# Thirty of 2,346 gathered tiles fetched row by row on SP's queue

## The chip, the core and the metric

The kernel runs on one core of one Trainium2 chip. The metric is the device time of one execution in microseconds (us). The kernel before was run three times: 2960.32, 2960.99 and 2961.77 us, median 2960.99.

## What is computed

The reference is a three-layer graph network over 6,250 nodes of 256 features and 100,000 edges in three relations, and the edges are sorted by their destination. Cut to what matters:

```
ew = edge_attr @ edge_w + edge_b                        # 100000 x 256, the same in all layers
for l in range(3):
    msg = relu(x[src] * ew)                             # one gathered row of x for each edge
    out = x @ roots[l] + biases[l]
    for i in range(3):
        h = segment_sum(msg * (type == i)[:, None], dst, n) * inv_cnt[i][:, None]
        out = out + h @ weights[l, i]
    x = x + relu(out)
result = layernorm(x_in + x)
```

The expression `x[src]` is the point of the change: in each layer 100,000 rows of 1 KB are read from DRAM at addresses that only the data tells. Layer 0 reads them from the input x, layers 1 and 2 from `x_mid`, the layer's input that the layer before wrote to DRAM.

## The kernel before, in words

The edges are cut into tiles of 128, one edge in each partition: 782 tiles a layer. Two tiles are a pair, two pairs a quad; a layer has 391 pairs. The order of the pairs is a list, `order`: pairs 64 to 390 first, then 63 down to 0. The kernel is written as a hand-made software pipeline (`layer`, from L587): a loop over steps `it`, one pair a step, in which each kind of work on a pair is issued at a fixed distance. Every engine keeps the order in which its instructions are written.

- **Gather**, nine steps ahead (AHEAD, called `gather`). `gather_pair` (L1051) issues one indirect DMA for each tile from GpSimd (POOL): 128 rows by 128 indices, L1054. The quad's four tiles go to one of eight rooms of a ring (`rows`, ROWS = 8). The first six pairs of a layer are fetched at the end of the layer before, from a copy of the nodes in which one node tile is still missing, and completed later.
- **Edge weights**, five steps ahead: TensorE (PE) multiplies the edge attributes with `edge_w` (L634). The attributes come by `load_at`, a 256 KB load from SP's queue for every eight pairs (L571), into three rooms.
- **Messages**, three steps ahead: VectorE (DVE) multiplies the gathered quad with the weights (L656), ScalarE (ACT) takes the relu (L657).
- **Sums**, at the step itself: PE multiplies the messages with one-hot matrices (L687, L695), DVE adds the result into an accumulator (`add`, L723) at a place that is loaded into registers, eight at once (L716). After that the quad's room is free.
- **Nodes**: when all edges of a node tile (128 nodes) are in, PE multiplies its sums with the weights (`node_mul`, L754), DVE ends it (`node_end`, L785, L788) and SP stores it to `x_mid` (L791), in the last layer to the output (L808). The first of these node tiles come some 15 steps apart, the last ones four.

So SP's queue holds the attribute loads, the weight loads, in the last layer loads of the input (L815), and the stores. It waits at each store until DVE has made it.

At the start of layer 0 ACT's queue loads the biases and zeroes parts of the accumulator, writes zeros to `x_mid` (L526) and loads the node features six tiles at a time (`load_x`, L557), the first of them ahead of the loop. At step 20 `find_came` and `find_rows` (L574, L580) make the index tables of the later layers.

Of the kernel before, what the change touches and what calls it, by code (L numbers as in the profile page):

```python
# [442 lines left out]
def ordered_path(ctx, tc, x, attr_laid, A, weights, roots, biases, edge_w, edge_b, out, src, src_i, seg, place_i, consts, x_root,  # L443
# [6 lines left out]
    nc = tc.nc  # L450
    P = 128
    N, D = x.shape
    E = src.shape[0]
# [9 lines left out]
    order, _, _, least, most = schedule(N, E, 1)  # L463
# [15 lines left out]
    big = ctx.enter_context(tc.tile_pool(name="big", bufs=1))  # L479
# [47 lines left out]
    src_r = big.tile(list(src_i.shape), I32, name="src_r")  # L527
    src_e = big.tile([P, 2 * FIRST], I32, name="src_e")
    came = big.tile([P, 2 * FIRST, P], F32, name="came")
    came_i = came.bitcast(I32)  # L530

    edge = ctx.enter_context(tc.tile_pool(name="edge", bufs=2))
    rows = ctx.enter_context(tc.tile_pool(name="rows", bufs=ROWS))
    wpool = ctx.enter_context(tc.tile_pool(name="wpool", bufs=1))
    o_pool = ctx.enter_context(tc.tile_pool(name="o_p", bufs=1, space=PSUM))
    r_pool = ctx.enter_context(tc.tile_pool(name="r_p", bufs=1, space=PSUM))
# [3 lines left out]
    def first_of(p, n):  # L540
        return p == 0 or order[p - 1] // n != order[p] // n
# [8 lines left out]
    def closes(u):  # L550
        p = order.index(u)
        return p == U - 1 or span_of[order[p + 1]] != span_of[u]

    def load_x(c0):
        n = min(6, NT - 1 - c0)
        if n > 0:
            nc.scalar.dma_start(x_all[:, c0:c0 + n, :], x[c0 * P:(c0 + n) * P, :].rearrange("(c p) d -> p c d", p=P))  # L557
        if c0 + 6 >= NT - 1:
            last = N - (NT - 1) * P
            nc.scalar.dma_start(x_all[:last, NT - 1, :], x[N - last:, :])  # L560
# [13 lines left out]
    def find_rows():  # L574
        mine = src_i[:, 2 * order[0]:2 * (order[0] + FIRST)]
        for to, of, there in ((src_r, src_i, N + P), (src_e, mine, N)):
            nc.vector.tensor_scalar(to, of, float(P), float(there), op0=ALU.is_lt, op1=ALU.mult)
            nc.vector.scalar_tensor_tensor(to, of, float(-P), to, op0=ALU.add, op1=ALU.add)

    def find_came():  # L580
        e = 2 * P * order[0]
        nc.scalar.dma_start(came_i.rearrange("p t e -> p (t e)"),
                            src[e:e + 2 * FIRST * P][None, :].to_broadcast([P, 2 * FIRST * P]))
        for t in range(2 * FIRST):
            nc.vector.tensor_scalar(came[:, t, :], came_i[:, t, :], node_i[:, 0:1], None, op0=ALU.is_equal)

    def layer(l, r_sb, b_sb, ats, early, pools):  # L587
# [4 lines left out]
        _, starts, moved, _, _ = schedule(N, E, share)  # L592
# [9 lines left out]
        seen, h_bank = [0], {}  # L602

        def gather(u):
            p = order.index(u)
            if p < FIRST:
                xs[u // 2] = early[u // 2]
            else:
                if first_of(p, 2):
                    xs[u // 2] = room(rows, D)  # L610
                gather_pair(nc, xs[u // 2], x_rows, src_i if l == 0 else src_r, u)

        def pairs_of(q):
            return range(min(2, U - 2 * q))
# [207 lines left out]
        for j, c in enumerate(turns_of):  # L822
            step = max(3 + int((U - 110) * (1 - (1 - j / NT) ** 0.5)), max(root_at, default=-1) + 6)
            if j >= ROOTS:
                step = max(step, starts[turns_of[j - ROOTS]] + 5)
            assert step + 8 <= starts[c]
            root_at[step] = c
        for it in range(-11, max(starts) + 8):
            def pair(k):
                return order[it + k] if 0 <= it + k < U else None  # L830
            if pair(AHEAD) is not None:
                gather(pair(AHEAD))
            if l < L - 1 and 0 <= it + AHEAD - U < FIRST:
                gather_early(it + AHEAD - U)
            if l == 0 and it == 20:
                find_came()
                find_rows()
            if pair(AHEAD) is not None and pair(AHEAD) // GROUP not in ats:
                ats[pair(AHEAD) // GROUP] = load_at(pair(AHEAD) // GROUP)
            if l == 0 and it >= -4 and (it + 4) % 20 == 0 and (it + 4) // 20 * 6 < NT - 1:  # L840
                load_x((it + 4) // 20 * 6)
            if it == 10:
                nc.sync.dma_start(w_sb, weights[l].rearrange("r (c p) e -> p (r c) e", p=P))
            if l == L - 1 and it + 2 in root_at:
                load_x0(root_at[it + 2])
            if l < L - 1 and it == U - 10:
                r_next = load_root(l + 1)
            if l < L - 1 and U - 10 <= it < U - 8:
                ats_next[at_groups[it - U + 10]] = load_at(at_groups[it - U + 10])

            if pair(0) is not None:
                reduce(pair(0))
            for span in take_at.get(it, ()):
                take(span)
            if pair(5) is not None and first_of(it + 5, 2):
                make_ew(pair(5) // 2)
            for span in turn_at.get(it, ()):
                turn(span)
            if pair(3) is not None and first_of(it + 3, 2):
                if l > 0 and it + 3 < FIRST:  # L860
                    complete(pair(3) // 2)
                if pair(3) // 2 != order[-1] // 2:
                    weigh(pair(3) // 2)

            if pair(3) is not None and pair(3) // 2 == order[-1] // 2:
                k = pair(3) % 2
                if pair(3) == order[-1]:
                    weigh_last(pair(3) // 2, k)
                else:
                    weigh(pair(3) // 2, range(k, k + 1))  # L870
            if pair(6) is not None and first_of(it + 6, 2):
                seed_ew(pair(6) // 2)
            if it - 6 in root_at:
                root_keep(root_at[it - 6])
            if it in root_at:
                root_turn(root_at[it])
            if it - 2 in root_at:
                root_turned(root_at[it - 2])
            if it - 3 in root_at:
                root_mul(root_at[it - 3])  # L880
            if it == moved:
# [47 lines left out]
OCT = 4  # L929
PARTS = 3  # L930
FIRST = 6

ASTRAY = 1024

# [113 lines left out]
    return rows.tile([128, 2, 2, D], F32, name="xs", bufs=ROWS)  # L1048


def gather_pair(nc, xs, x_rows, src_i, u, u0=0):  # L1051
    for i in range(2):
        t = 2 * (u - u0) + i
        nc.gpsimd.indirect_dma_start(  # L1054
            out=xs[:, u % 2, i, :], out_offset=None, in_=x_rows[:, :],
            in_offset=bass.IndirectOffsetOnAxis(ap=src_i[:, t:t + 1], axis=0))
# [169 lines left out]
```

## Time and profile before

| | |
|---|---|
| Median of three runs | 2960.99 us |
| Profiled execution, its own time | 2962.1 us |
| Span of the profiled execution, first to last instruction | 2959.9 us |
| Mean granted TensorE clock | 0.972 |
| Busy share of PE, DVE, ACT, POOL | 87%, 68%, 51%, 75% |
| Indirect DMAs of L1054 on POOL | 12 + 770 + 24 + 1540 = 2,346 |
| Mean rate of all DMA | 131 GB/s |

How to read it: the profile lists busy time by engine; a share says how much of the span the engine worked and not whether it holds the others up. Instructions that set registers, wait or issue a DMA do not count as busy; they are listed under the names of the sequencers, SPq, ACTq, POOLq and DVEq. An indirect DMA counts on POOL with the time in which POOL makes its descriptors, and not with the time in which the rows travel. In a row of a timeline the last part, in brackets, is how long the engine was idle before the instruction and what ended that.

### The profile page before, as it was taken

The page shows a single profiled execution, that of the slowest core. Times are in us where ns is not written, and L with a number is a line of the kernel's source. Part 1 is how long each engine was busy: PE and PEld are TensorE (multiplying, and loading weights), DVE is VectorE, ACT ScalarE, POOL GpSimd, SP SyncE. Part 2 cuts the span into 40 slices and gives each one's busy share as a digit, 9 for nine tenths or more (in the row PEclk, how much of TensorE's full clock was granted, in tenths as well). Part 3 has the DMA queues.
Part 4 walks back from the last instruction along what each step waited for, and adds up shares of the span by engine and source line. Part 5 has one row for each costly group of instructions (what it writes and reads, how often), then busy time and mean ns, then how long its engine had stood idle before and what let it go on. Part 6 is the DMA issues. An engine that isn't in the chain of part 4 may idle for free. (4 is left out here: it accounts for less than half of the span.)

```text
span 2959.9 us, 43407 instructions
## 1 busy us (share of the span) xinstructions
PE 2585.9 (87%) x13712; PEld 1779.5 (60%) x13712; DVE 1999.4 (68%) x4910; ACT 1503.9 (51%) x1911; POOL 2227.8 (75%) x2355
## 2 busy tenths in 40 slices
PE   5999999999998778888889998778888988999876
PEld 2566677677765545556666666455555666666644
DVE  6666677778775555566767776545566777888864
ACT  4666666566565444454444444434444444444443
POOL 7777777777777777777777777777777777777776
PEclk9999999999999999999999999989999999999998
DMA  5444444444444444444444444444444444444443
GB/s 168 146 146 136 148 124 124 129 131 129 129 133 130 132 116 120 129 122 123 127 125 130 131 131 129 135 132 125 125 133 134 135 132 132 138 136 139 129 127 96
DMA packets 173705, 387.39 MB, mean 131 GB/s; under 512 B 43594, under 2 KB 79068, under 8 KB 173468
## 3 DMA queue, kind: packets, MB, share of 16 engines
q0 software_dynamic: 112608, 307.65, 36.4%
q1 hardware_dynamic: 53280, 68.50, 7.2%
q10 hardware_dynamic: 7580, 8.37, 1.0%
q8 instruction: 113, 1.85, 0.3%
q14 instruction: 124, 1.02, 0.1%
HBM read 364.89 MB, written 19.46 MB: 130 GB/s over the span
## 5 line engine op out<-in xcount | busy, mean ns | idle before, releaser
L1054 POOL DMA_INDIRECT xs<-x_mid,src_r x1540 | 1460.3, 948 | 469.1 <-issue 360.0
L657 ACT ACTIVATE xs<-xs 128x1024 f32<-128x1024 f32 (+1 forms) x585 | 615.7, 1052 | 1290.2 <-DVE xs L656 1269.8
L656 DVE TENSOR_TENSOR xs<-ew_p,xs 128x1024 f32<-128x1024 f32 (+1 forms) x585 | 711.8, 1217 | 662.0 <-DMA xs<-x_mid,src_r 433.4
L1054 POOL DMA_INDIRECT xs<-in_x_dram,src_io x770 | 731.2, 950 | 235.4 <-issue 196.8
L695 PEld LDWEIGHTS h_p<-oh,xs 128*128 128x128 f32 x5160 | 665.1, 195 | 253.7 <-issue 122.5
L695 PE MATMUL h_p<-oh,xs 128*128 128x120 f32 x5160 | 728.9, 286 | 88.7 <-issue 38.2
L634 PE MATMUL ew_p<-ew_sb,at 64*128 64x512 f32 x2346 | 688.5, 663 | 106.0 <-ACT ew_p L621 101.1
L669 DVE TENSOR_SCALAR oh<-iota_w,seg_o 128x120 f32<-128x120 f32 x2346 | 623.5, 328 | 0.0
L687 PE MATMUL h_p<-xs,oh 128*120 128x256 f32 x2088 | 571.7, 408 | 21.4 <-issue 7.4
L621 ACT ACTIVATE ew_p<-seed 128x1024 f32<-128x1024 f32 x582 | 588.8, 1012 | 0.0
L754 PE MATMUL o_p<-w_sb,acc 128*128 128x256 f32 (+1 forms) x1728 | 440.1, 391 | 30.5 <-DVE x_root L785 27.4
L687 PEld LDWEIGHTS h_p<-xs,oh 128*120 128x120 f32 x2088 | 363.7, 192 | 163.1 <-issue 50.0
L723 DVE TENSOR_TENSOR acc<-h_p,acc 128x240 f32 (+1 forms) x732 | 324.6, 443 | 184.8 <-PE o_p L754 67.9
L754 PEld LDWEIGHTS o_p<-w_sb,acc 128*128 128x128 f32 (+1 forms) x1728 | 309.4, 191 | 152.2 <-DVE x_root L785 67.3
L634 PEld LDWEIGHTS ew_p<-ew_sb,at 64*128 64x128 f32 x2346 | 182.0, 189 | 234.7 <-ACT ew_p L621 131.0
L785 DVE SCALAR_TENSOR_TENSOR x_root<-o_p,inv,x_root 128x256 f32<-128x256 f32 (+1 forms) x432 | 207.3, 480 | 27.6 <-PE o_p L754 20.9
L736 PE MATMUL r_p<-r_sb,t_s 128*128 128x256 f32 x588 | 160.8, 397 | 25.3 <-ACT t_s L732 25.0
L771 ACT ACTIVATE acc<-zero_o 128x768 f32<-128x768 f32 (+1 forms) x150 | 140.2, 935 | 15.2 <-PE o_p L754 14.6
L673 ACT ACTIVATE oh_b<-oh 128x480 bf16<-128x480 f32 x196 | 116.4, 594 | 59.0 <-DVE oh L669 58.1
L736 PEld LDWEIGHTS r_p<-r_sb,t_s 128*128 128x128 f32 x588 | 104.6, 195 | 46.2 <-ACT t_s L732 34.5
L728 PEld LDWEIGHTS r_p<-ident_o,x_all 128*128 128x128 f32 x294 | 30.6, 143 | 160.9 <-DVE x_root L739 107.1
L728 PE MATMUL r_p<-ident_o,x_all 128*128 128x128 f32 x294 | 65.1, 304 | 62.9 <-DVE x_root L739 62.1
(110 smaller groups left out, 939.3 us busy)
## 6 DMA issues: line engine op xcount, KB each, us to landing
at<-in_attr_laid_dram SPq DMA_DIRECT2D x147, 256.0 KB
xs<-x_mid,src_r POOLq DMA_INDIRECT x1540
xs<-in_x_dram,src_io POOLq DMA_INDIRECT x770
x_mid<-x_all SPq DMA_DIRECT2D x96, 128.0 KB
x_all<-in_x_dram ACTq DMA_DIRECT2D x8, 768.0 KB
x<-in_x_dram SPq DMA_DIRECT2D x48, 128.0 KB
out_dram<-x_all SPq DMA_DIRECT2D x48, 128.0 KB
w_sb<-in_L_gnn_weights_dram SPq DMA_DIRECT2D x3, 768.0 KB
```

The lines of the kernel that those rows point to most:

```text
L621: nc.scalar.activation(ew_ps[q][:, :n], seed[:, None, :, :].to_broadcast([P, n, 2, D]), AF.Copy)
L634: nc.tensor.matmul(ew_ps[q][:, k].rearrange("p i d -> p (i d)"), at[half, :], ew_sb[half].rearrange("p i d -> p (i d)"), start=False, stop ...
L656: nc.vector.tensor_mul(there, ew_ps[q][:, pairs.start:pairs.stop], there)
L657: nc.scalar.activation(there, there, AF.Relu)
L669: nc.vector.tensor_scalar(ohs[q][:, i, :], iota_w[:, :, :WIN], seg[:, 4 * q + i:4 * q + i + 1], None, op0=ALU.is_equal)
L687: nc.tensor.matmul(h_p[:WK, :D], ohs[u // 2][:, t, :], xs[u // 2][:, u % 2, i, :], start=(i == 0 and first), stop=(i == 1 and closes(u)), ...
L695: nc.tensor.matmul(h_p[:, d * WK:(d + 1) * WK], xs[u // 2][:, u % 2, i, d * P:(d + 1) * P] if d < DC else full_ones, (ohs if d < DC else o ...
L723: nc.vector.tensor_tensor(there, h_ps[span][:, :CH * WK].rearrange("p (c r w) -> p c r w", c=CH, r=R), there, op=ALU.add)
L736: nc.tensor.matmul(rs[c][:, 1, :], t_ss[c][:, d, :], r_sb[:, d, :], start=(d == 0), stop=(d == DC - 1))
L754: nc.tensor.matmul(o_p[:n, j, :], acc[:, d, r, slot:slot + n], w_sb[:, r * DC + d, :], start=(d == 0), stop=(d == DC - 1))
L785: nc.vector.scalar_tensor_tensor(root, o_p[:n, j, :], inv[:n, c, r:r + 1], root, op0=ALU.mult, op1=ALU.add)
L1054: nc.gpsimd.indirect_dma_start(out=xs[:, u % 2, i, :], out_offset=None, in_=x_rows[:, :], in_offset=bass.IndirectOffsetOnAxis(ap=src_i[:, ...
```

## The change

Ten quads in each layer, about 36 steps apart, get their fourth tile in another way. `singles` lists them. POOL gathers only the first three tiles of such a quad, into one of two new rooms (`slow`, tile `xs_s`) instead of one of the eight. The 128 rows of the fourth tile are fetched one by one from SP's queue, four a step over 32 steps, with four steps of rest. For each step `single_rows` writes four loads of one row (1 KB, into one partition), whose address is a register; at every second step eight indices are first loaded from SBUF into SP's registers. The last four rows of a tile are written four steps ahead of the multiply that reads them.

At the start `find_singles` loads the indices of these ten tiles by ten small loads on ACT's queue and makes the second table, for layers 1 and 2, by two operations on DVE. The diff, cut to its core:

```
+    singles = []
+    for j in range(SINGLES):
+        p = EVERY * (j + 1)
+        while not (first_of(p, 2) and 4 * (order[p] // 2) + 4 <= E // P):
+            p += 1
+        singles.append(order[p] // 2)
+
+    def find_singles():
+        for j, q in enumerate(singles):
+            e = (4 * q + 3) * P
+            nc.scalar.dma_start(src_s[j:j + 1, 0, :], src[e:e + P][None, :])
+        nc.vector.tensor_scalar(src_s[:, 1], src_s[:, 0], float(P), float(N + P), op0=ALU.is_lt, op1=ALU.mult)
+        nc.vector.scalar_tensor_tensor(src_s[:, 1], src_s[:, 0], float(-P), src_s[:, 1], op0=ALU.add, op1=ALU.add)
...
-                if first_of(p, 2):
+                if first_of(p, 2) and u // 2 not in singles:
                     xs[u // 2] = room(rows, D)
-                gather_pair(nc, xs[u // 2], x_rows, src_i if l == 0 else src_r, u)
+                gather_pair(nc, xs[u // 2], x_rows, src_i if l == 0 else src_r, u,
+                            tiles=(0,) if u // 2 in singles and u % 2 else (0, 1))
+
+        def single_rows(it):
+            j, at = divmod(it + 2, EVERY)
+            if j < 0 or j >= SINGLES or AT_ONCE * at >= P:
+                return
+            q = singles[j]
+            if at == 0:
+                xs[q] = slow.tile([P, 2, 2, D], F32, name="xs_s")
+            if at % 2 == 0:
+                e = AT_ONCE * at
+                _, found[:] = nc.values_load_multi_w_load_instructions(
+                    src_s[j:j + 1, min(l, 1), e:e + 2 * AT_ONCE], engines=[mybir.EngineType.SP], min_val=0,
...
+            for k in range(AT_ONCE):
+                e = AT_ONCE * at + k
+                r = nc.s_assert_within(found[e % (2 * AT_ONCE)], 0, x_rows.shape[0] - 1,
...
+                nc.sync.dma_start(xs[q][e:e + 1, 1, 1, :], x_rows[bass.ds(r, 1), :])
...
+        if l == 0:
+            find_singles()
         for it in range(-11, max(starts) + 8):
...
+            single_rows(it)
...
+SINGLES = 10
+EVERY = 36
+AT_ONCE = 4
```

Three places show what stands in the queues. The first is POOL's queue over layer 0, before and then after; `x_root` and `xs` are rooms of gathered rows, `src_f`, `src_io`, `src_e` and `src_r` index tables, and the number behind an x counts equal instructions in a row.

```order
L1054 DMA x_root<-in_x_dram,src_f 128x256 x12
L1171 TENSOR_LOAD flag
L1172 COMPARE_AND_BRANCH
L1054 DMA xs<-in_x_dram,src_io 128x256 x770
L1054 DMA xs<-x_mid_226,src_e 128x256 x12
L1054 DMA xs<-x_mid_226,src_r 128x256 x770
```

```order
L1097 DMA x_root<-in_x_dram,src_f 128x256 x12
L1214 TENSOR_LOAD flag
L1215 COMPARE_AND_BRANCH
L1097 DMA xs<-in_x_dram,src_io 128x256 x60
L1097 DMA xs_s<-in_x_dram,src_io 128x256 x3
L1097 DMA xs<-in_x_dram,src_io 128x256 x68
L1097 DMA xs_s<-in_x_dram,src_io 128x256 x3
```

Nothing is added or reordered on POOL; after every 68 gathers (60 the first time) come three into a room `xs_s`, where four stood before.

The second place is SP's queue in layer 0, at its first store of a node tile, before and then after; `at` is a room of attributes, and the brackets name the semaphores on which an instruction waits, DMAHW0 to DMAHW7 being those of the loads and stores of SP and ACT.

```order
L571 DMA at_1061<-in_attr_laid_dram 128x512 [waits DMAHW4_49,DMAHW1_49,PE_49]
L571 DMA at_1241<-in_attr_laid_dram 128x512 [waits DMAHW5_49,DMAHW2_49,PE_49]
L791 DMA x_mid0_226<-x_all_267 128x256 [waits DMAHW0_49,DMAHW3_49,DVE_49,Pool_49]
L571 DMA at_1384<-in_attr_laid_dram 128x512 [waits DMAHW7_49,PE_49]
L791 DMA x_mid0_226<-x_all_267 128x256 [waits DVE_49]
```

```order
L648 DMA xs_s_1390<-in_x_dram 1x256 [waits DMAHW4_49]
L588 DMA at_1832<-in_attr_laid_dram 128x512 [waits DMAHW5_49,PE_49]
L828 DMA x_mid0_226<-x_all_267 128x256 [waits DMAHW6_49,DVE_49,Pool_49]
L641 TENSOR_LOAD src_s_285
L648 ISA
L648 DMA xs_s_1390<-in_x_dram 1x256 [waits DMAHW7_49]
L648 ISA
L648 DMA xs_s_1390<-in_x_dram 1x256 [waits DMAHW0_49]
L648 ISA
L648 DMA xs_s_1390<-in_x_dram 1x256 [waits DMAHW1_49]
```

The row loads stand between the loads and stores that were there. Each is one register operation (ISA, two multiplications fused) and one DMA, with one TENSOR_LOAD of eight registers for eight rows, and each waits for the DMA that used the same one of the eight semaphores before it, so that at most eight are under way.

The third place is ACT's queue at the start of layer 0, before and then after; `x_all` holds the node features, `src_s` the indices of the ten tiles.

```order
L520 ACTIVATE acc<-zero_o 128x4080 x2
L526 DMA x_mid_226<-x_all 128x256
L526 DMA x_mid_227<-x_all 128x256
L557 DMA x_all<-in_x_dram 128x6x256
L657 ACTIVATE x_root<-x_root 128x1024
```

```order
L526 DMA x_mid1_227<-x_all_267 128x256 [waits DMAHW7_49]
L567 DMA src_s_285<-in_src_dram 1x128 [waits DMAHW0_49]
L567 DMA src_s_285<-in_src_dram 1x128 [waits DMAHW1_49]
L567 DMA src_s_285<-in_src_dram 1x128 [waits DMAHW2_49]
L567 DMA src_s_285<-in_src_dram 1x128 [waits DMAHW3_49]
L567 DMA src_s_285<-in_src_dram 1x128 [waits DMAHW4_49]
L567 DMA src_s_285<-in_src_dram 1x128 [waits DMAHW5_49]
L567 DMA src_s_285<-in_src_dram 1x128 [waits DMAHW6_49]
L567 DMA src_s_285<-in_src_dram 1x128 [waits DMAHW7_49]
L567 DMA src_s_285<-in_src_dram 1x128 [waits DMAHW0_49]
L567 DMA src_s_285<-in_src_dram 1x128 [waits DMAHW2_49]
L574 DMA x_all_267<-in_x_dram 128x6x256 [waits DMAHW4_49]
```

The ten loads stand ahead of the first load of node features. The sixth waits on DMAHW5, which the first attribute load of SP (L588) used just before, and the two DVE operations that read `src_s` stand ahead of DVE's first multiply.

More of the change, by code (lines that the diff above doesn't have):

```diff
@@ L530, in ordered_path @@
     came_i = came.bitcast(I32)
+    src_s = big.tile([SINGLES, 2, P], I32, name="src_s")
     edge = ctx.enter_context(tc.tile_pool(name="edge", bufs=2))
     rows = ctx.enter_context(tc.tile_pool(name="rows", bufs=ROWS))
+    slow = ctx.enter_context(tc.tile_pool(name="slow", bufs=2))
     wpool = ctx.enter_context(tc.tile_pool(name="wpool", bufs=1))
@@ L601, in layer @@
         r_next, ats_next, early_next = (None, None), {}, {}
-        seen, h_bank = [0], {}
+        seen, h_bank, found = [0], {}, []
         def gather(u):
@@ L608, in gather @@
             else:
-                if first_of(p, 2):
+                if first_of(p, 2) and u // 2 not in singles:
                     xs[u // 2] = room(rows, D)
-                gather_pair(nc, xs[u // 2], x_rows, src_i if l == 0 else src_r, u)
+                gather_pair(nc, xs[u // 2], x_rows, src_i if l == 0 else src_r, u,
[11 more added lines that the diff above has]
+                    src_s[j:j + 1, min(l, 1), e:e + 2 * AT_ONCE], engines=[mybir.EngineType.SP], min_val=0,
+                    max_val=x_rows.shape[0] - 1, skip_runtime_bounds_check_because="it is a node's row")
+            for k in range(AT_ONCE):
+                e = AT_ONCE * at + k
+                r = nc.s_assert_within(found[e % (2 * AT_ONCE)], 0, x_rows.shape[0] - 1,
+                                       skip_runtime_bounds_check_because="it is a node's row")
+                nc.sync.dma_start(xs[q][e:e + 1, 1, 1, :], x_rows[bass.ds(r, 1), :])
         def pairs_of(q):
@@ L1048, in room, with gather_pair @@
     return rows.tile([128, 2, 2, D], F32, name="xs", bufs=ROWS)
-def gather_pair(nc, xs, x_rows, src_i, u, u0=0):
-    for i in range(2):
+def gather_pair(nc, xs, x_rows, src_i, u, u0=0, tiles=(0, 1)):
+    for i in tiles:
         t = 2 * (u - u0) + i
```

## The prediction

> **What bounds the kernel now.** I read the shares of the page first, then the groups of instructions, the waits of each engine, and the timeline of POOL. The page names PE as the busiest engine, but that is no bound by itself:
>
> ```profile
> PE 2585.9 (87%) x13712; PEld 1779.5 (60%) x13712; DVE 1999.4 (68%) x4910; ACT 1503.9 (51%) x1911; POOL 2227.8 (75%) x2355
> ```
>
> The gathers of POOL, by their line (minimum, median and maximum in ns, then the start of the first and the last in us):
>
> ```profile
> L1054 POOL DMA_INDIRECT xs<-x_mid,src_r x1540: 942/946/1404, 1000.8 to 2944.0; - x193
> L1054 POOL DMA_INDIRECT xs<-in_x_dram,src_io x770: 942/946/2052, 19.1 to 984.4; - x193
> L1054 POOL DMA_INDIRECT xs<-x_mid,src_e x24: 942/946/1091, 985.7 to 1977.8; - x24
> L1054 POOL DMA_INDIRECT x_root<-in_x_dram,src_f x12: 942/946/1103, 3.9 to 17.9; - x12
> ```
>
> There are 12 + 770 + 24 + 1540 = 2,346, from 3.9 to 2944.0 us: (2944.0 − 3.9) / 2345 = 1.2538 us from one to the next. The timeline shows that this is no average over bursts and pauses; its columns are start, duration, instruction, and in brackets the idle time before it:
>
> ```profile
> 55.49 0.95 POOL L1054 DMA_INDIRECT xs<-in_x_dram,src_io  x1 [0.30 <-issue]
> 56.74 0.94 POOL L1054 DMA_INDIRECT xs<-in_x_dram,src_io  x1 [0.30 <-issue]
> 57.99 0.95 POOL L1054 DMA_INDIRECT xs<-in_x_dram,src_io  x1 [0.30 <-issue]
> 60.04 0.95 POOL L1054 DMA_INDIRECT xs<-in_x_dram,src_io  x1 [1.11 <-ACT t_s L732]
> ...
> 2942.78 0.95 POOL L1054 DMA_INDIRECT xs<-x_mid,src_r  x1 [0.30 <-issue]
> 2944.03 0.95 POOL L1054 DMA_INDIRECT xs<-x_mid,src_r  x1 [0.30 <-issue]
> ```
>
> Each takes 0.95 us and 0.30 us pass before the next. The waits of POOL (total, times, longest) say the same for the whole span:
>
> ```profile
> POOL xs L1054 <- issue: 563.2, 1849, 0.3
> POOL xs L1054 <- ACT t_s L732: 6.6, 19, 1.1
> ```
>
> The 0.30 us is POOL's own pace. Only once, at 60 us, did it wait for a room, 0.8 us beyond that. So POOL issues gathers without a pause from 4 us to 2944 us, and what follows the last one takes 2959.9 − 2944.0 = 15.9 us. The other engines follow it: DVE waits for gathered rows. Its waits in layer 1 (990 to 1970 us) and late in layer 0 (700 to 860 us) are headed by:
>
> ```profile
> DVE xs L656 <- DMA xs<-x_mid,src_r: 253.9, 138, 4.4
> ...
> DVE acc L723 <- PE o_p L754: 11.1, 5, 3.3
> ```
>
> In layer 1 DVE waited 138 times for rows. Late in layer 0 no such wait is listed: the consumers are behind there, yet not so far that POOL found no room.
>
> **The gathers that go.** Thirty of 2,346: 30 × 1.2538 = 37.6 us, if POOL stays the bound. The DMA engines are no obstacle to that: 0.4 to 0.5 of their time is taken.
>
> ```profile
> DMA  5444444444444444444444444444444444444443
> q0 software_dynamic: 112608, 307.65, 36.4%
> q1 hardware_dynamic: 53280, 68.50, 7.2%
> q10 hardware_dynamic: 7580, 8.37, 1.0%
> ```
>
> On the page "DMA: Bandwidth & Descriptors" the Trainium skill speaks against the change (section "Issuing engines are not separate DMA queues"): all DMAs run on the same 16 engines whichever engine starts them, and starting them elsewhere saves only sequencer time, usually little. By that rule taken alone the gain is nothing and the time 2961 us; the trace differs, since here it is the 1.25 us of issuing on POOL that sets the pace.
>
> **The rows on SP.** Before, SP's queue mostly waits. Now it has 3,840 row loads besides, and the question is what one costs it. The nearest rows:
>
> ```profile
> L791 SPq DMA_DIRECT2D x_mid<-x_all x98: 247/320/331, 147.9 to 1971.5; - x98
> L571 SPq DMA_DIRECT2D at<-in_attr_laid_dram x147: 327/383/1116, 33.2 to 2884.5; - x147
> L483 ACTq DMA_DIRECT2D ew_sb<-in_L_gnn_edge_w_dram x4: 432/436/443, 20.3 to 21.7; - x4
> L716 DVEq TENSOR_LOAD <-place_i x135: 593/596/1055, 60.5 to 2888.8; - x135
> L723 DVEq FUSED_REGOPS  x729: 69/69/69, 61.2 to 2889.5; - x183
> L1171 SPq FUSED_REGOPS  x1: 186/186/186, 16.7 to 16.7; - x1
> ...
> 33.15 1.29 SPq L571 DMA_DIRECT2D at<-in_attr_laid_dram  x3
> ```
>
> No DMA of one row is in the trace. From below, 0.25 us is the shortest on SP, a store; from above, 0.44 us is the median of loads that follow each other at once on ACT. I take 0.32 us, the median store, because one row is less work than any of these. The register operation is 0.07 us as on DVE, or 0.19 us as in SP's only case; its two multiplications are nearer to DVE's. Eight registers cost 0.60 us, 0.075 us a row. Between two instructions of a queue I put 0.05 us, since three loads take 1.29 us where three medians are 1.15; two gaps a row are 0.10 us. Sum: 0.32 + 0.07 + 0.075 + 0.10 = 0.57 us a row; lowest 0.25 + 0.07 + 0.075 + 0.10 = 0.50 us, highest 0.44 + 0.19 + 0.075 + 0.10 = 0.80 us.
>
> What SP has for it: 36 steps of two gathers less one are 71 × 1.2538 = 89 us. In them stand 4.5 attribute loads of 0.38 us and, where nodes end every fourth step, some eight stores of 0.32 us: 4.3 us. A tile's rows take 128 × 0.57 = 73 us. Sum 77 of 89 us, so SP keeps up. The turning point is (89 − 4.3) / 128 = 0.66 us a row, inside my bounds. Eight transfers in flight do not set a lower pace: a gather lands 2.75 us after its issue, as the chain that ended last shows, and 2.75 / 8 = 0.34 us.
>
> ```profile
> 2944.03 2.75 DMA xs<-x_mid,src_r
> SPq L791 <- DVE x_all L788: 1431.2, 87, 46.3
> ```
>
> The second row, from SP's own waits, is why SP cannot run far ahead: it stands at each store until DVE has made it, and the row loads behind it now stand too. They are released at DVE's own step, and have four steps, 10 us, until DVE needs the last of them. At 0.57 us a step's four rows take 2.3 us where a step takes 2.5, so nothing piles up. If it did, DVE would wait at the quad's multiply; POOL would go on until the eight rooms, 16 pairs or 40 us of gathers, were full.
>
> **The start.** The ten loads on ACT push the first load of node features back by 10 × 0.44 = 4.4 us, which nothing needs early. More matters that the sixth waits until the first attribute load has landed, and that DVE cannot multiply before all ten are in:
>
> ```profile
> 38.33 2.17 PE L634 MATMUL ew_p<-ew_sb,at 64*128 64x512 f32 x4 [4.15 <-DMA at<-in_attr_laid_dram]
> 40.53 1.23 DVE L656 TENSOR_TENSOR x_root<-ew_p,x_root 128x1024 f32<-128x1024 f32 x1 [7.41 <-PE ew_p L634]
> L578 DVE SCALAR_TENSOR_TENSOR src_e<-src_io,src_e x1: 170/170/170, 92.3 to 92.3; 128x12 int32<-128x12 int32 x1
> ```
>
> The first attributes, issued in the row of three loads above, are used at 38.3 us. That means that five more loads are issued until 40.5 and land, by the 2.75 us of a gather, at 43.3; two operations of 0.17 us follow, and the first multiply starts at 43.6 instead of 40.5. On the other side the first attribute load no longer shares its way with two others and a weight load, and may land up to 2 us sooner. POOL stands at the edge of its rooms just then, so a delay of the consumers shows: 0 to 3 us. I take 1 us. Later attribute loads stand behind up to 32 rows, 18 us, of which the three attribute rooms cover most.
>
> Extra waits on DVE, PE and ACT for the ten quads I cost at nothing: DVE's 254 us of waiting in layer 1 hide them.
>
> **The sum.** Against the profiled execution, 2962.1 us (span 2959.9 and 2.2 us around it): 2962.1 − 37.6 + 1 = 2925.5 us. The median of the runs is 1.1 us below the profiled execution: **2924 us**, and 2920 to 2935 us for this case alone.
>
> **Rivals.** *SP becomes the bound (slower).* Above 0.66 us a row SP falls back at every tile, and DVE and then POOL wait for it. At 0.72 us a tile takes 128 × 0.72 + 4.3 = 96.5 us, 7.5 us too long; ten tiles less the 10 us of lead make 65 us a layer, 195 us in all: 2924 + 195 = 3119 us. For it speaks SP's 0.19 us of register operations, and the 0.44 us of loads without a pause; against it that the stores, the smallest DMAs on SP, take 0.32. Chance 0.17. Close above the turning point, at 0.68 us, the loss is 91.3 − 89 a tile, 13 us a layer after the lead, 40 us in all, and cancels the gain: 2964 us, or 2957 to 2966 us: chance 0.05.
>
> *One DMA engine becomes the bound (slower).* A load into one partition cannot be spread as 128 are. If all rows go through one engine, it has its 45% (36.4, 7.2 and 1.0% of the three queues) of 2960 us, 1320 us, and 3,840 rows besides. A packet of q1 takes 0.072 × 16 × 2960 / 53280 = 0.064 us, one of q0 0.153 us; with two packets a row that is 490 to 1180 us, a load of 61 to 85%. Only from (2924 − 1320) / 3840 = 0.42 us a row does it decide; at 0.45 us the time is 1320 + 1728 = 3048 us. Chance 0.03. The rule behind it is on the same page of the Trainium skill (section "Why a DMA increments its semaphore by 16 and not by 1"): the number of engines divides the outermost size, and one partition gets one, the lowest-numbered. No row of before shows which engine a packet took.
>
> *The consumers become the bound in layer 0.* If POOL's ten gathers there buy nothing, 20 × 1.2538 = 25 us remain: 2961 − 25 + 1 = 2937 us. For it speaks that DVE does not wait for rows from 700 to 860 us; against it that POOL was never held up there. Chance 0.13.
>
> **How the numbers follow.** The forecast has 0.62, the consumers 0.13, the balance 0.05, SP 0.17, the one engine 0.03. Faster by more than 0.2%, about what a measurement of this kernel can tell from no change: 0.75; within it 0.05; slower 0.20. The range holds the first three cases: 2920 to 2966 us.
>
> **What would show it.** Right: L1054's successor on POOL has 2,316 gathers 1.25 us apart, the last at some 2907 us; SP's row loads take 0.3 us and start 0.57 us apart; DVE's multiplies of `xs_s` do not wait for them. Wrong: DVE waits for `xs_s` at many of the thirty quads, POOL's idle time before a gather grows beyond 0.3 us in steady state, or gathers stay as many.

## The result, and the profile after

The changed kernel takes 2925.71 us in the median (2924.25 to 2926.22), the kernel before 2961.09 us on the same chip: a ratio of 0.9879, 95% interval 0.9867 to 0.9891, faster by 35.4 us. The profiled execution took 2925.2 us, with a span of 2923.1 us and a clock of 0.976.

The shares of the page, and two of its queues, show what went and what came:

```profile
PE 2570.1 (88%) x13712; PEld 1774.4 (61%) x13712; DVE 1999.4 (68%) x4912; ACT 1505.4 (51%) x1911; POOL 2199.7 (75%) x2325
q0 software_dynamic: 111168, 303.71, 36.3%
q1 hardware_dynamic: 60960, 72.45, 8.1%
```

POOL has thirty instructions fewer, and q1, which carries SP's transfers, 7,680 packets more: two for each of 3,840 rows, one of 1,024 bytes and one of 4.

The gathers of POOL after the change (minimum, median and maximum in ns; start of the first and the last in us):

```profile
L1097 POOL DMA_INDIRECT xs<-x_mid,src_r x1460: 942/946/1637, 988.0 to 2906.9; - x183
L1097 POOL DMA_INDIRECT xs<-in_x_dram,src_io x730: 940/946/2003, 19.1 to 971.7; - x183
L1097 POOL DMA_INDIRECT xs_s<-x_mid,src_r x60: 942/946/954, 1063.7 to 2836.9; - x60
L1097 POOL DMA_INDIRECT xs_s<-in_x_dram,src_io x30: 942/946/1142, 95.3 to 901.7; - x30
L1097 POOL DMA_INDIRECT xs<-x_mid,src_e x24: 942/946/948, 973.0 to 1953.2; - x24
L1097 POOL DMA_INDIRECT x_root<-in_x_dram,src_f x12: 942/946/1103, 3.9 to 17.9; - x12
```

They are 2,316, and (2906.9 − 3.9) / 2315 = 1.2540 us apart: the pace of before, with thirty steps fewer. The early gathers (`src_e`) stand at the seams of the layers. Their first starts at 973.0 us (985.7 before), their last at 1953.2 us (1977.8 before), so each layer gave about ten gathers: 12.7, 11.9 and 12.5 us, 37.1 us in all.

The rows on SP, in the same columns; the store and the attribute load behind them are those that were there before:

```profile
L648 SPq FUSED_REGOPS  x3840: 37/37/48, 34.6 to 2827.9; - x192
L648 SPq MOVE xs_s<-x_mid x2560: 29/29/29, 983.9 to 2827.9; - x197
L648 SPq DMA_DIRECT2D xs_s<-x_mid x2560: 224/228/337, 984.0 to 2828.0; - x197
L641 SPq TENSOR_LOAD <-src_s x480: 544/784/1511, 34.0 to 2824.1; - x160
L828 SPq DMA_DIRECT2D x_mid<-x_all x98: 251/373/382, 150.6 to 1947.7; - x98
L588 SPq DMA_DIRECT2D at<-in_attr_laid_dram x147: 327/363/410, 33.5 to 2847.7; - x147
```

A row is three instructions, not two: a register operation (0.037 us), a MOVE that was not foreseen (0.029 us) and the DMA (0.228 us). SP's timeline (start, duration from first to last, instruction, count) gives the pace with everything in it:

```profile
104.89 0.37 SPq L588 DMA_DIRECT2D at<-in_attr_laid_dram  x1
106.21 11.47 SPq L648 DMA_DIRECT2D xs_s<-in_x_dram  x24
117.77 0.37 SPq L588 DMA_DIRECT2D at<-in_attr_laid_dram  x1
```

Between the two attribute loads stand 24 rows with their register loads. Without the 0.42 us of the first of these loads and the gap behind it that is 117.77 − 104.89 − 0.42 = 12.46 us, so 0.52 us a row. Summed over eight tiles of layer 1, each instruction counted up to the start of the next, a row costs 0.533 us: DMA 0.284, register operation 0.077, MOVE 0.063, an eighth of a TENSOR_LOAD 0.109.

Who waits now (total in us, times, longest): the engines for rows and for what stands behind them on SP, and then SP's own waits:

```profile
DVE xs L693 <- DMA xs<-x_mid,src_r: 399.2, 216, 4.5
DVE xs_s L693 <- DMA xs_s<-in_x_dram: 4.2, 2, 2.6
DVE xs_s L693 <- DMA xs_s<-x_mid: 3.7, 5, 1.5
PE ew_p L671 <- DMA at<-in_attr_laid_dram: 20.9, 6, 8.4
```

```profile
SPq L828 <- DVE x_all L825: 294.6, 58, 32.3
SPq L648 <- DMA x_all<-in_x_dram: 33.1, 8, 8.8
```

DVE hardly waits for SP's rows (7.9 us in seven places). SP still has 294.6 us in which it stands at these stores, 1431.2 before. PE's 20.9 us of waiting for attributes, all in layer 0, stand against 4.1 us in the kernel before:

```profile
PE ew_p L634 <- DMA at<-in_attr_laid_dram: 4.1, 1, 4.1
```

New are 33.1 us in which row loads of SP wait for the loads of node features that ACT issues: both use the same eight semaphores in turn.

### The profile page after: what moved, and what is told of

It is laid out like the page before. It is cut to its first block, busy times and chain, and to the rows that moved or that the text cites. A ratio compares the mean times of both kernels' runs of the same rounds, so it can differ in the third digit from the quotient of the medians.

```text
span 2923.1 us, 55840 instructions
## 1 busy us (share of the span) xinstructions
PE 2570.1 (88%) x13712; PEld 1774.4 (61%) x13712; DVE 1999.4 (68%) x4912; ACT 1505.4 (51%) x1911; POOL 2199.7 (75%) x2325
## 5 line engine op out<-in xcount | busy, mean ns | idle before, releaser
L1097 POOL DMA_INDIRECT xs<-x_mid,src_r x1460 | 1385.2, 949 | 445.0 <-issue 353.0
L694 ACT ACTIVATE xs<-xs 128x1024 f32<-128x1024 f32 x555 | 584.0, 1052 | 1184.4 <-DVE xs L693 1153.9
L693 DVE TENSOR_TENSOR xs<-ew_p,xs 128x1024 f32<-128x1024 f32 x555 | 674.8, 1216 | 570.7 <-DMA xs<-x_mid,src_r 399.2
L1097 POOL DMA_INDIRECT xs<-in_x_dram,src_io x730 | 693.1, 949 | 223.1 <-issue 185.3
L671 PE MATMUL ew_p<-ew_sb,at 64*128 64x512 f32 x2346 | 680.0, 655 | 117.7 <-ACT ew_p L658 96.1
L732 PEld LDWEIGHTS h_p<-oh,xs 128*128 128x128 f32 x4848 | 627.9, 196 | 224.7 <-issue 115.6
L732 PE MATMUL h_p<-oh,xs 128*128 128x120 f32 x4848 | 688.3, 287 | 66.6 <-issue 29.6
L724 PE MATMUL h_p<-xs,oh 128*120 128x256 f32 x2004 | 539.1, 402 | 14.3 <-issue 7.4
L724 PEld LDWEIGHTS h_p<-xs,oh 128*120 128x120 f32 x2004 | 344.3, 189 | 145.2 <-issue 45.7
L808 ACT ACTIVATE acc<-zero_o 128x768 f32<-128x768 f32 (+1 forms) x150 | 140.2, 935 | 15.6 <-PE o_p L791 14.9
```

The costliest lines, as they stand in the source:

```text
L671: nc.tensor.matmul(ew_ps[q][:, k].rearrange("p i d -> p (i d)"), at[half, :], ew_sb[half].rearrange("p i d -> p (i d)"), start=False, stop ...
L693: nc.vector.tensor_mul(there, ew_ps[q][:, pairs.start:pairs.stop], there)
L694: nc.scalar.activation(there, there, AF.Relu)
L724: nc.tensor.matmul(h_p[:WK, :D], ohs[u // 2][:, t, :], xs[u // 2][:, u % 2, i, :], start=(i == 0 and first), stop=(i == 1 and closes(u)), ...
L732: nc.tensor.matmul(h_p[:, d * WK:(d + 1) * WK], xs[u // 2][:, u % 2, i, d * P:(d + 1) * P] if d < DC else full_ones, (ohs if d < DC else o ...
L1097: nc.gpsimd.indirect_dma_start(out=xs[:, u % 2, i, :], out_offset=None, in_=x_rows[:, :], in_offset=bass.IndirectOffsetOnAxis(ap=src_i[:, ...
```

## The experiments

Twelve runs on four chips. Each ratio is against the kernel before on the same chip, which took 2968.0 us for the first four runs and 2961.3 us for the next four; in the traces GpSimd's gathers took 0.949 us in the median on the first of these chips (0.946 in the run with doubled rows) and 0.946 us on the second. The times that are expected below count from 2961 us for the kernel before, so on the first chip the ratios are what to compare.

**The gathers alone (e1_static).** The kernel before, with

```
-                gather_pair(nc, xs[u // 2], x_rows, src_i if l == 0 else src_r, u)
+                gather_pair(nc, xs[u // 2], x_rows, src_i if l == 0 else src_r, u,
+                            tiles=(0,) if u // 2 in singles and u % 2 else (0, 1))
+                if u // 2 in singles and u % 2:
+                    nc.sync.dma_start(xs[u // 2][:, 1, 1, :], x_rows[0:P, :])
```

> The kernel before with 30 of GpSimd's gathers left out, at the places where the change leaves them out, and no row fetched in their place: SP loads the first 128 rows of the source in one transfer for each (30 transfers), so these 30 tiles hold other rows than the reference's and the output differs. It prices the 30 gathers alone. Theory (GpSimd's pace of 1.254 us a gather sets the end, the rows on SP cost nothing): 30 x 1.254 = 37.6 us off the time of before, 2923 us (2921 to 2927), the changed kernel's 2925.7 within 3 us. Rival one (the rows do cost something, by the DMA engines or by stores that they delay, and the gain is what is left): 2910 to 2920, below the changed kernel by that cost. Rival two (the gain comes from SP, not from the gathers): about 2961, no gain.

Measured: 2932.7 us, ratio 0.988 (0.9863 to 0.9896). That is the changed kernel's ratio, as the theory had it. This run's gathers serve as a measure for two of the next three runs:

```profile
L1066 POOL DMA_INDIRECT xs<-x_mid,src_r x1520: 945/949/1397, 991.1 to 2913.0; - x190
L1066 POOL DMA_INDIRECT xs<-x_mid,src_e x24: 945/949/950, 976.1 to 1957.7; - x24
```

Layer 0 ends at 976.1 us, layer 1 takes 981.6 and layer 2 takes 955.3 us. The gain is that of the thirty gathers, and the rows take nothing from it that this measurement can tell.

**The rows alone (e2_rows_extra).** The changed kernel, with

```
-                if first_of(p, 2) and u // 2 not in singles:
+                if first_of(p, 2):
...
-                            tiles=(0,) if u // 2 in singles and u % 2 else (0, 1))
...
-                nc.sync.dma_start(xs[q][e:e + 1, 1, 1, :], x_rows[bass.ds(r, 1), :])
+                nc.sync.dma_start(spare[q][e:e + 1, 1, 1, :], x_rows[bass.ds(r, 1), :])
```

> The changed kernel with GpSimd gathering all 2,346 tiles into the ring as in the kernel before; SP still fetches its 3,840 rows, into its two rooms, which nobody reads. It prices the rows alone. Theory (rows beside the gathers are free, SP at 0.515 us a row stays in its 36 steps): 2961 to 2962 us, no change from before. Rival one (the rows take time of the DMA engines or of the stores that wait behind them on SP): above 2965. Rival two (the gain came from somewhere else than the 30 gathers): about 2926.

Measured: 2972.5 us, ratio 1.0013 (1.0004 to 1.0023): 4.5 us slower than before, 1.2 to 6.8 by the interval. With the thirty gathers back the gain is gone, so it came from them. The rows cost a little after all, which is what the first rival says. Where they do it is not shown for certain; PE's waits, and one pause of POOL, point to layer 0:

```profile
PE ew_p L670 <- DMA at<-in_attr_laid_dram: 16.0, 6, 8.3
98.72 0.95 POOL L1096 DMA_INDIRECT xs<-in_x_dram,src_io  x1 [3.08 <-issue]
```

PE's waits are all in layer 0, as in the changed kernel, and the pause is 2.8 us longer than POOL's usual 0.30 us. So the rows are not quite free: the first two runs together leave their cost at a few us at most.

**Toward SP's limit (e3_twice).** Every second row is fetched a second time:

```
+                if e % 2:
+                    nc.sync.dma_start(twice[e:e + 1, :], x_rows[bass.ds(r, 1), :])
```

> The changed kernel with every second row of SP's fetched a second time, into a scratch tile that nobody reads: 192 DMA instructions a tile in place of 128. It moves SP toward the point at which it no longer keeps up. The trace of the changed kernel shows 0.411 us from row to row inside a group of eight and 0.515 us as the mean of a row; a second DMA adds between 0.26 us (its 0.228 and a gap) and 0.41 us, so a row's mean becomes 0.645 to 0.72 us, and 128 of them and the stores (4.3 us) need 87 to 96 us of the 89 us that a tile has. Theory (SP becomes the bound above 0.66 us a row): at 0.645 no change, 2926 us; at 0.72 7.5 us too long a tile, 65 us a layer after the lead of 10 us, 3119 us; the middle, 0.68, about 2960 to 3000. Rival (SP is not what decides, the rows could wait): 2926 at any of these.

Measured: 3302.0 us, ratio 1.1117 (1.1099 to 1.1136). SP is the bound, and by more than was expected: a repeat cost 0.418 us, since it too is a register operation, a MOVE and a DMA, where 0.26 to 0.41 had been reckoned. SP's queue waits for DVE at the stores of `x_mid` for 78.3 us in place of 294.6, and PE waits behind it:

```profile
SPq L831 <- DVE x_all L828: 78.3, 18, 25.1
```

```profile
PE ew_p L674 <- DMA at<-in_attr_laid_dram: 456.8, 83, 14.9
DVE xs_s L696 <- DMA xs_s<-x_mid: 33.9, 8, 7.4
```

What SP's lateness costs is not so much the rows' own multiply as the attribute loads that stand behind the rows: 457 us of PE's time against 45 us of DVE's (33.9, and 10.9 in layer 0). In layer 1 tiles follow each other on SP every 100.5 us. The instructions there sum up to 0.742 us for a row and its half of a repeat, 95.0 us a tile, and 5.5 us for stores and attribute loads. So SP has no rest left. The granted clock was lower in this run, 0.904 where the changed kernel had 0.976, but the sum fills the tile without it. A tile has 71 gathers, 89.2 us at the pace of the first run; 11.3 us too long, ten times, less the lead of 10 us, is 103 us. The gathers tell how long the layers took:

```profile
L1100 POOL DMA_INDIRECT xs<-x_mid,src_r x1460: 940/946/1654, 1153.4 to 3281.9; - x183
L1100 POOL DMA_INDIRECT xs<-x_mid,src_e x24: 942/946/949, 1134.1 to 2214.2; - x24
```

Layer 1 took 2214.2 − 1134.1 = 1080.1 us, against 981.6 in the first run: 98.5 us more; layer 2 112 us more. Layer 0 lost 158 us; its tiles came every 106 us, and row loads there also wait for the loads of node features (32.8 us). So the prediction's rule, excess times tiles less the lead, comes near in layers 1 and 2 once the time of a tile from SP's own instructions is put in.

**Twelve tiles (e4_every32).**

```
-SINGLES = 10
-EVERY = 36
+SINGLES = 12
+EVERY = 32
...
-            j, at = divmod(it + 2, EVERY)
+            j, at = divmod(it + 6, EVERY)
```

> Twelve tiles a layer in place of ten, one every 32 steps in place of 36, and each tile's rows begun four steps earlier, still four a step: six gathers fewer on GpSimd over three layers. SP needs 128 x 0.515 + 4.3 = 70 us of the 32 x 2.46 = 79 us. Theory (GpSimd's pace is still the bound): 6 x 1.254 = 7.5 us less than the changed kernel, 2918 us (2915 to 2921). Rival one (SP decides already: fewer rests between tiles): above 2930. Rival two (something else than the gathers now bounds the end, the consumers of the tiles): 2924 to 2927, no further gain.

Measured: 2946.5 us, ratio 0.9930 (0.9912 to 0.9947), slower than the changed kernel, as the first rival has it. The theory failed in this run, and only in layer 0:

```profile
L1097 POOL DMA_INDIRECT xs<-x_mid,src_r x1444: 945/949/1645, 1006.0 to 2925.2; - x181
L1097 POOL DMA_INDIRECT xs<-x_mid,src_e x24: 945/949/951, 991.0 to 1971.2; - x24
```

```profile
SPq L648 <- DMA x_all<-in_x_dram: 32.1, 8, 6.8
```

```profile
PE ew_p L671 <- DMA at<-in_attr_laid_dram: 40.6, 14, 7.1
```

Layer 0 ended at 991.0 us, 14.9 us after the first run's 976.1, with two gathers fewer. Layers 1 and 2 took 980.2 and 954.0 us, 1.4 and 1.3 us less than there, of the 2.5 us that two gathers are worth. In layer 0 SP can begin only at 34 us, when the row numbers have come, and waits 32 us for node loads. With a tile every 32 steps (63 gathers, 79 us) the rows of one tile began some 1 us after those of the last ended, here as in the other layers. But in layer 0 the lateness of the start stayed: its first six tiles began 79.5 us apart, and the last row of the first five was issued only 2.0 to 2.8 us before DVE's multiply, in layers 1 and 2 always 5 us or more. The attribute loads came late, and 39.0 of PE's 40.6 us lie in this layer. This is not the whole account: the pauses of POOL in layer 0, beyond its usual 0.30 us between gathers, sum up to 20.7 us, and 11.1 us of them came after 400 us, when no row waited for a node load any more. No run separates the causes.

**Later tiles (e5_late), and the changed kernel beside it (e8_again).**

```
-        p = EVERY * (j + 1)
+        p = EVERY * (j + 1) + LATE
...
-            j, at = divmod(it + 2, EVERY)
+            j, at = divmod(it + 2 - LATE, EVERY)
+LATE = 6
```

> The changed kernel once more, on the chip of the three runs beside it, so that they can be compared with it directly. Every theory: 0.988 of the kernel before (0.9867 to 0.9891 in its first timing), some 2925 us.

> The changed kernel with every tile of SP's six steps (15 us) later in the order, and its rows as much later; as many tiles, rows and gathers. In the changed kernel the last row of tiles 0 to 3 of layer 0 is issued 2.0 to 2.4 us before the tile's multiply, in all others 3.4 to 17 us before; VectorE waits 7.9 us for rows there. Theory (SP decides in the first tiles of layer 0, because its rows can begin only at 34.8 us, when the row numbers have come): VectorE's waits for rows go, 1 to 4 us less than the changed kernel, about 2923 us. Rival (these waits are hidden behind GpSimd's pace): within 1 us of it.

Measured: 2925.6 us for the changed kernel, ratio 0.988 (0.9865 to 0.9895), and 2925.6 us with later tiles, 0.9878 (0.9863 to 0.9894). With later tiles:

```profile
PE ew_p L671 <- DMA at<-in_attr_laid_dram: 17.1, 5, 7.9
DVE xs_s L693 <- DMA xs_s<-x_mid: 1.6, 1, 1.6
```

DVE's waits for SP's rows fell to 1.6 us, from 7.9 in the first trace of the changed kernel and 8.4 in the one beside this run, and nothing that the timing can tell came of it: the rival. PE's waits for attributes stayed (18.6 us in the run beside it).

**Denser where SP has room (e6_mixed12).** Layer 0 as in the run with later tiles, and for layers 1 and 2 a second list and table:

```
+FEW = 10, 36, 4, 2, 6
+MORE = 12, 32, 4, 6, 0
...
+        SINGLES, EVERY, AT_ONCE, lead, late = FEW if l == 0 else MORE
```

> Layer 0 as in the run with later tiles (ten, every 36 steps, six steps later); layers 1 and 2 with twelve tiles, every 32 steps, begun four steps earlier. Twelve tiles in every layer gave 2946 us beside 2968 of before: layer 0 ended about 18 us late (its early gathers began at 991.0 us, not 973.0), layers 1 and 2 took 980.2 and 954.0 us, against 980.2 and 953.7 of the changed kernel on a chip whose gathers were 0.0025 us apart nearer (2 us a layer). Theory (in layer 0 SP is late, by its start and by 32 us of waits for the node loads' semaphores; in layers 1 and 2 GpSimd's pace is the bound): the 18 us don't come back, and 4 gathers fewer give 5.0 us: 2917 to 2922 us, 3 to 8 us below the changed kernel. Rival one (denser rows cost as much in layers 1 and 2 as they save): within 2 us of the run with later tiles. Rival two (12 tiles are too many in any layer): above 2935.

Measured: 2920.1 us, ratio 0.9862 (0.9847 to 0.9877), the fastest of all. The interval overlaps that of the changed kernel beside it, so the timing alone shows no more than that it is not slower; the traces show what was gained:

```profile
L1102 POOL DMA_INDIRECT xs<-x_mid,src_r x1444: 942/946/1319, 988.0 to 2900.8; - x181
L1102 POOL DMA_INDIRECT xs<-x_mid,src_e x24: 942/946/949, 973.0 to 1950.5; - x24
```

Layers 1 and 2 took 977.5 and 950.3 us, in the changed kernel beside it 979.7 and 953.1: 5.0 us for four gathers, as reckoned. Layer 0 ended within 1 us of the other, although SP's rows waited 54.4 us for node loads there: with ten tiles a layer there is room for that.

**Thirteen tiles (e7_mixed13).** `MORE = 13, 29, 5, 5, 0`: five rows a step, and ten row numbers read at a time.

> The same with thirteen tiles in layers 1 and 2, every 29 steps, five rows a step. SP needs 128 x 0.515 + 4.3 = 70 us and 1.5 us for the attribute loads, of 29 x 2.46 = 71.3 us: just at the point where it should no longer keep up. Theory (SP's own instructions set the turning point): six gathers fewer give at most 7.5 us and SP's lateness takes some back: 2914 to 2926 us; in the trace the rows of one tile follow those of the last without rest and SP hardly waits for VectorE. Rival (a hidden limit lies nearer than SP's sum): above 2930. Other rival (SP's need is smaller than the sum): 2914 to 2918, with rests left.

Measured: 3196.8 us, ratio 1.0793 (1.0778 to 1.0808), on the side of the first rival. Again the sum had a wrong term, this time the register load:

```profile
L646 SPq TENSOR_LOAD <-src_t x338: 719/1394/2985, 984.4 to 3153.3; - x169
L646 SPq TENSOR_LOAD <-src_s x160: 557/788/1132, 34.6 to 915.7; - x160
```

```profile
L1102 POOL DMA_INDIRECT xs<-x_mid,src_r x1436: 940/946/1490, 990.2 to 3165.3; - x180
L1102 POOL DMA_INDIRECT xs<-x_mid,src_e x24: 942/945/948, 975.2 to 2067.5; - x24
```

```profile
PE ew_p L676 <- DMA at<-in_attr_laid_dram: 436.8, 76, 12.6
```

Eight numbers took 0.79 us in layer 0; in layers 1 and 2 loads of ten took 1.21 and 2.34 us by turns, with the gap behind them 1.80 us in the mean, 23.4 us a tile in place of 13.9. In layer 1 a tile came every 81.6 us where it had 57 gathers, 71.4 us, and SP stood still for 1 to 4 us of it (gaps over 0.15 us): 13 × 10.2 − 10 = 123 us by the prediction's rule. Layer 1 took 115 us more than in the run before, layer 2, where a tile came every 83.4 us, 148 us more. The bill is PE's again, through the attribute loads.

**Thirteen tiles, reads of eight and of sixteen (e9_eights13, e10_sixteens13, and once more as e11_eights13 and e12_sixteens13).**

```
+            for e in range(AT_ONCE * at, min(AT_ONCE * (at + 1), P)):
+                if e % 8 == 0:
...
+                        src_of[j:j + 1, min(l, 1), e:e + 8], engines=[mybir.EngineType.SP], min_val=0,
```

(16 in place of 8 in the other).

> Thirteen tiles in layers 1 and 2 as in the last run (every 29 steps, five rows a step), but the row numbers are read into registers eight at a time, from multiples of eight, as in the changed kernel. In the last run ten were read at a time, and the TENSOR_LOADs alternated between 1.2 and 2.3 us (0.78 us for eight in the changed kernel); 13 of them took some 23 us of a tile's 80, in place of the 12.6 us that were reckoned. Theory (that alone made the last run 3197 us; the sum of SP's instructions sets the turning point): SP needs 71.7 us of the 71.3 that a tile has, at the point itself; six gathers fewer give at most 7.5 us, and lateness of up to 1 us a tile beyond the lead takes some back: 2915 to 2930 us. Rival (thirteen tiles are too many for another reason: stores and attribute loads that SP issues late, which the consumers wait for): above 3000, near the last run.

> The same with sixteen row numbers read at a time, from multiples of sixteen: eight TENSOR_LOADs a tile. From the run with ten at a time (1.2 us where they cross a boundary of 32 bytes, 2.3 us where they cross one of 64) a load of sixteen should take 1.2 us, estimated, and cross no boundary of 64. Theory: a tile needs 128 x 0.411 + 8 x 1.25 + 5.8 = 68.4 us of 71.3; SP keeps up with rests, 2915 to 2920 us, below the changed kernel by 6 to 9 us. Rival (the load's time grows with the number of registers, 2.3 us or more for sixteen): a tile needs 77 us or more, above 3050.

> The kernel with eights once more, since the chip of its first timing took 3664 us for the kernel before (2961 to 2968 on the others), with register operations of SP that took 0.037 us elsewhere at 0.34 us in the slowest tenth. Theory as there: a tile needs 71.7 us of SP of the 71.3 that it has; 2915 to 2930 us where the kernel before takes 2961, a ratio of 0.985 to 0.990, and a row read of eight at 0.78 us. Rival (thirteen tiles are too many for another reason than the reads of ten): a ratio above 1.01.

> The kernel with sixteens once more, for the same reason. Its reads took 1.22 us in the median there, as estimated. Theory: a tile needs 68.4 us of SP of 71.3, SP keeps up with rests: 2915 to 2920 us where the kernel before takes 2961, a ratio of 0.984 to 0.986, the lowest of all. Rival (thirteen tiles are too many for another reason): a ratio above 1.01.

Measured, in this order: 4241.4, 4194.5, 4153.4 and 4123.4 us, ratios 1.1572 (1.1537 to 1.1606), 1.1452 (1.1413 to 1.1490), 1.1494 (1.1459 to 1.1529) and 1.1422 (1.1376 to 1.1468). On the two chips that ran them the kernel before itself took 3663.8 and 3606.3 us in place of 2961 to 2968, at a clock near 0.88. Single instructions of SP were spread there as on no other chip, here in the third run (its register operation took 37 to 48 ns elsewhere) and the fourth:

```profile
L651 SPq FUSED_REGOPS  x4608: 1/37/1396, 43.2 to 4125.3; - x192
```

```profile
L646 SPq TENSOR_LOAD <-src_t x208: 12/1228/2776, 1331.1 to 4078.7; - x104
```

So these four runs do not tell whether thirteen tiles pay where the kernel before takes 2961 us: the ratio above 1.01 that the rival asked for came about on chips that neither theory spoke of, and why these were slow stays open. Tiles came every 103 to 108 us in layer 1, but also every 121 to 124 us in layer 0, which has only ten; whether a kernel that keeps SP near its limit loses more on such a chip is not shown. One thing they do show: a read of sixteen took 1.23 us in the median.

## Why the prediction was right

**The bound.** POOL's pace was the limit, 1.2538 us forecast and 1.2540 measured; the last gather was forecast at some 2907 us and started at 2906.9. The first run shows that thirty gathers less, with no row fetched one by one, give the same ratio, and the second that the rows without this bring no gain. The Trainium skill says that issuing from several engines saves only sequencer time, usually little beside the DMA itself (page "DMA: Bandwidth & Descriptors", section "Issuing engines are not separate DMA queues"). The trace agrees with the first half and not with the second: what was saved is sequencer time, but here it was the bound. Thirty gathers of it are 37.6 us by the pace; the spans of the two traces differ by 36.8 us and the medians by 35.4 us, with 32 to 39 us as the interval.

**A row on SP.** Right in size, 0.533 us against 0.57, inside 0.50 to 0.80 (the expectations above reckon with 0.515), but out of parts that were off both ways, so that some of the closeness is luck. The DMA itself took 0.228 us, below the 0.25 that I held for the lower end; the register operation 0.037, half of DVE's; the MOVE of 0.029 and its gap were not in the sum; the register load was 0.784, not 0.60, and its eighth with the gap 0.109, not 0.075. A tile needed 128 × 0.533 + 4.3 = 72.5 us, 77 forecast, of the 89.

**The start.** The sum's 1 us is of the right order, but the delay that it stands for did not occur. DVE did wait for the ten index loads, as the prediction says, yet its first multiply was not delayed from 40.5 to 43.6 us:

```profile
36.43 1.45 ACTq L567 DMA_DIRECT2D src_s<-in_src_dram  x5
36.55 2.17 PE L671 MATMUL ew_p<-ew_sb,at 64*128 64x512 f32 x4 [2.03 <-DMA at<-in_attr_laid_dram]
39.66 0.21 DVE L568 TENSOR_SCALAR src_s<-src_s 10x128 int32<-10x128 int32 x1 [6.20 <-DMA src_s<-in_src_dram]
39.91 0.28 DVE L569 SCALAR_TENSOR_TENSOR src_s<-src_s 10x128 int32<-10x128 int32 x1
40.12 1.22 DVE L693 TENSOR_TENSOR x_root<-ew_p,x_root 128x1024 f32<-128x1024 f32 x1
```

It started at 40.1 us. The first attributes were used at 36.6 us in place of 38.3, inside the "up to 2 us sooner" of the prediction, so the sixth index load could go at 36.4 us. The five last loads then took 1.45 us of ACT, 2.2 reckoned, and had landed 1.8 us later, 2.75 reckoned. What the change costs comes later in layer 0, through attribute loads behind waiting rows: the second run puts it at 4.5 us (1.2 to 6.8), forecast 0 to 3. In the changed kernel itself the gathers lose less, 2315 × (1.2540 − 1.2538) = 0.5 us against the pace of before.

**SP as the bound.** The mechanism is real, and the changed kernel is on the safe side of it, as forecast. At 36 steps a tile the runs put the turning point between 0.533 us a row, where the gathers keep their pace, and 0.742, where they do not; 0.66 itself was not tried. Two steps of this rival failed. The stall was put at DVE's multiply of the late quad; the runs put it at PE, which waits for attribute loads, and the sentence that the three attribute rooms cover most of that holds only while SP keeps up. And the sum behind the turning point leaves out what layer 0 has besides: rows that can begin only at 34 us, and some 33 us in which they wait for node loads that share their semaphores. There twelve tiles, with a sum of 73 of 79 us, were already too many, for these or for other reasons. The lead of 10 us was not there everywhere either: in the changed kernel the last row of the first four tiles of layer 0 was issued 2.0 to 2.4 us before the tile's multiply, in the others 3.4 to 17 us.

**The other rivals.** Layer 0 gave its 12.7 us, so its consumers were not the bound. One DMA engine as the bound would have shown in the pace of the gathers, which did not change. A row was not spread: each added one packet of 1,024 bytes and one of 4. In the trace's list of packets those of 1,024 bytes took 219.6 us more than before and those of 4 bytes 34.6 us more, 0.066 us a row, where the rival reckoned with 0.13 to 0.31 us; even if all went through one engine, that is some 1570 of its 2924 us, an estimate. Which engine took them the trace does not show.

## What to carry to other kernels

Where one engine's issue rate is the bound and another engine's queue mostly waits, work moved over was worth its slots in full here, as far as the timing can tell, as long as the receiving queue kept rests; price it by all of its instructions, register loads and moves too. Then ask what else stands in that queue: when it fell behind, the loss came through attribute loads that another engine waited for, not through the rows that were moved. And take the room stage by stage: the same density that gained 5 us in layers 1 and 2 lost 15 us in layer 0.

## What the runs showed of the hardware

- **A register load's time went with where it starts.** Counted in bytes within the tile's row, on SP TENSOR_LOADs of eight registers from multiples of 32 bytes took 0.79 us, of sixteen from multiples of 64 bytes 1.23 us. Loads of ten took 1.21 us where they began at a multiple of 16 bytes and 2.34 us where they began 8 bytes behind one. The expectation above laid the difference to boundaries that the loads cross; sorted by their start, the loads of that run fit the start and not the crossing. The two kinds alternate in every tile, and only this run has them; no run was made to test the start alone.
- **A small DMA on SP.** With its address in a register, a transfer of one row of 1 KB took 0.228 us of SP, a 128-row load 0.363 and a 128-row store 0.373.
- **Queues are coupled by semaphores.** SP's row loads waited up to 8.8 us in the changed kernel, and up to 11.2 us in the fastest run, for loads that ACT had issued and whose data they do not use: the two queues take the same eight semaphores in turn.
